# Layer 2's messages in two float32r parts instead of three bf16 parts, in a four-layer graph network

## The chip, the cores and the metric

The kernel runs on one core of a Trainium2 chip. The metric is the device time of one execution in microseconds; of several executions the median is taken. A core has a TensorE for matmuls, a VectorE, a ScalarE and a GpSimd for elementwise work, and queues of transfers (here all issued by SyncE) that move data between the core's own memory and the chip's large one. Each engine works through its instructions in the order in which the program lists them.

## What is computed

64 graphs of 256 nodes with 256 features each run through four layers. Each layer normalises its input, applies a ReLU, and adds its result to the input. Layers 0, 1 and 3 are forms of masked graph attention. Layer 2, which the change rewrites in part, is a gated graph network of three steps; `A` holds zeros and ones.

```python
# --- layer 2 (adj_preln) ---
h = jnp.maximum(_layernorm(x, axis=-1), 0.0)
x = x + _L2_gnn_ref(h, adj, L2_gnn_weight, L2_gnn_w_ih, L2_gnn_w_hh, L2_gnn_b_ih, L2_gnn_b_hh)
# ...
    def _gru_cell(inp, h, w_ih, w_hh, b_ih, b_hh):
        gi = inp @ w_ih.T + b_ih
        gh = h @ w_hh.T + b_hh
        # split in three; r, z sigmoids
        n = jnp.tanh(i_n + r * h_n)
        return (1.0 - z) * n + z * h
# ...
    A = (adj != 0).astype(x.dtype)
    h = x
    for i in range(3):
        m = jnp.einsum('bnd,de->bne', h, weight[i])
        aggr = jnp.einsum('bst,bsd->btd', A, m)
        h = _gru_cell(aggr, h, w_ih, w_hh, b_ih, b_hh)
    return h
```

## The kernel before

Two graphs form a pair, and the 32 pairs are the unit of work (T = 4 blocks of 128 nodes, P = 128, N = D = 256, N2 = 512). The Python program first collects tasks, each with an engine (or several to choose from), an assumed duration and the buffers it reads and writes. A planner then orders all tasks of all pairs by simulating the engines with these assumed durations, so that tasks of several pairs interleave on each engine. Among tasks that could begin at the same time, keys decide: in the kernel before, one key per layer for TensorE, for the transfers and for the others.

Layer 2 multiplies the adjacency first (`A.T h`) and folds the layer's weight into the input weights of the gates (`giT`). In the kernel before, the fp32 state `h` is split in three bf16 parts whose sum is `h`, so that each product with the zeros and ones of the adjacency is exact. The upper half of a float32 is a bf16, and so the stationary operand is read in place with a stride (`upper`).

```python
    def layer2(xt, p):
        at, hT, h = norm_relu_T(xt, p, tokens=True)
        am = buf("mask")
        add(
            (V, dve2(T * N), lambda: nc.vector.tensor_scalar(am(), at().bitcast(I32), 0.0, None, ALU.not_equal), True),
            reads=[hT, at], writes=[am],
        )
        at_o = lambda b, o: tok(b(), N2)[:, o, :]


        def upper(ap):
            return ap.bitcast(BF).rearrange("p (i h) -> p i h", h=2)[:, :, 1]

        def chunk_of(ap, mixed, t, o):
            if mixed:
                return upper(ap).rearrange("p (m x) -> p x m", x=2 * T)[:, T * o + t]
            return tok(upper(ap))[:, t, o * P : (o + 1) * P]

        def messages(h):
            rest = [w4(), w4()]
            add(
                (V, dve(T * N), lambda: nc.vector.tensor_tensor(
                    rest[0](), h(), upper(h()), ALU.subtract), True),
                reads=[h], writes=[rest[0]],
            )
            add(
                (V, dve(T * N), lambda: nc.vector.tensor_tensor(rest[1](), rest[0](), upper(rest[0]()), ALU.subtract), True),
                reads=[rest[0]], writes=[rest[1]],
            )
            aT = w4()
            for o in range(2):
                ps = bank()

                def product(o=o, ps=ps):
                    for g in range(2):
                        for i in range(3):
                            part = (h, *rest)[i]
                            for c in range(2):
                                t = 2 * g + c
                                mm(
                                    ps()[:, g * N : (g + 1) * N], chunk_of(part(), h.mixed, t, o), tok(am(), N)[:, t, :],
                                    start=i == 0 and c == 0, stop=i == 2 and c == 1,
                                )

                add((PE, 1.38, product), reads=[h, *rest, am], writes=[ps], claims=[aT])
                add(
                    evict(N2, lambda o=o: at_o(aT, o), ps),
                    reads=[ps], writes=[(aT, o)],
                )
            return aT
```

The gates are fp32 matmuls of 512 columns; each step has 24 of them:

```python
            def gate(us, terms, c0, o, claims=()):
                ps = bank()

                def do():
                    n = 0
                    for w, src in terms:
                        for k in range(2):
                            mm(ps(), w[:, k, c0 : c0 + P], wide(src, k), start=n == 0, stop=n == 2 * len(terms) - 1)
                            n += 1

                add((PE, us, do), reads=[*(src for _, src in terms), HH, *([GI[l]] if len(terms) > 1 or terms[0][0] is not whhT else [])], writes=[ps], claims=claims)
                return ps

            # ...
            for o in range(2):
                ps = gate(1.72, ((whhT, hT),), (4 + o) * P, o, [r, hn])
                # ... hn = 0.5 * ps + bias, on ScalarE or VectorE
            aT = messages(h)
            both = ((whhT, hT), (giT[:, l], aT))
            for o in range(2):
                ps = gate(3.44, both, o * P, o, [r])
                # ... tanh on ScalarE, then hn = (r + 1) * hn on VectorE
            for o in range(2):
                ps = gate(1.72, ((giT[:, l], aT),), (4 + o) * P, o, [u])
                # ... hn = tanh(ps + hn); u = hT - hn
            for o in range(2):
                ps = gate(3.44, both, (2 + o) * P, o)
                # ... tanh on ScalarE; u = 0.5 * (r + 1) * u + hn on VectorE
            hT = u
            h = w4()
            if by_dma(l, p):          # all pairs but the last one
                turn_chunks(u, h)
            # ... in the last pair: eight transposes on TensorE
```

After each step the new state lies with features on the partitions and must be turned. This goes through 32x32 transposes on VectorE and one write and four reads of the large memory, which leave the features in a mixed order:

```python
    def turn_chunks(src, dst):

        e = w4()
        add(
            (V, 1.8, lambda: nc.vector.transpose(
                e().rearrange("p (b i x) -> p b x i", b=4, i=32), src().rearrange("p (x b j) -> p b x j", b=4, j=32))),
            reads=[src], writes=[e],
        )
        through_dram(e, dst)
        dst.mixed = True

    # ...
    def through_dram(e, eT):

        d = buf("turn")
        add((SP, 0.6, lambda: nc.sync.dma_start(d(), e())), reads=[e], writes=[d], latency=4.6)
        for b in range(4):
            add(
                (SP, 0.55, lambda b=b: nc.sync.dma_start(
                    eT()[32 * b : 32 * b + 32, :].rearrange("p (a w) -> p a w", a=4),
                    d()[:, b * N : (b + 1) * N].rearrange("(a j) w -> j a w", a=4))),
                reads=[d], writes=[(eT, b)], latency=3.8,
            )
```

Of the kernel before, what the change touches and what calls it, by code (L numbers as in the profile page):

```python
# [9 lines left out]
FP = mybir.dt.float32  # L10
BF = mybir.dt.bfloat16
I32 = mybir.dt.int32
# [4 lines left out]
P = 128  # L17
# [17 lines left out]
class Task:  # L35
    __slots__ = ("pair", "forms", "bufs", "rank", "layer", "before", "after", "waits", "begin", "end", "engine", "latency", "rest", "key", "index")


class Plan:
# [14 lines left out]
    SPARE, GRAIN = 6, 0.001  # L54
# [4 lines left out]
    PERIOD, REST = 896, 0  # L59
    ON_PE = (-1435, -211, 9269, -4344)  # L60
    ON_SP = (6322, 2165, 5264, -1155)
    OTHERS = (224, 368, 701, 3083)

    def __init__(self, slots, spare):
        self.slots, self.spare = slots, spare
        self.pairs = []
        self.layer, self.rank = 0, None
# [4 lines left out]
    def add(self, forms, reads=(), writes=(), latency=0.0, claims=()):  # L72
# [11 lines left out]
        t.layer = self.layer  # L84
# [24 lines left out]

    def order(self):  # L110
# [11 lines left out]
        for t in reversed(every):  # L122
            t.rest = max((x.rest + 0.2 for x in t.after), default=0.0) + min(f[1] for f in t.forms) + t.latency
            base = t.rank[0] * self.PERIOD - t.rest * self.REST + t.rank[1] * 1e-4
            engine = t.forms[0][0]
            t.key = base + (self.ON_PE if engine == "PE" else self.ON_SP if engine == "SP" else self.OTHERS)[t.layer]
# [3 lines left out]
        free = {}  # L130
# [5 lines left out]
        while ready:  # L136
            best = None
            for t in ready:
# [8 lines left out]
                else:  # L147
                    for form in t.forms:
                        engine = form[0]
                        begin = max(start, free.get(engine, 0.0), free.get("port", 0.0) if len(form) > 3 else 0.0)  # L150
                        for x in t.before:
                            hop = self.HOP[x.engine] + (engine == "SP") * self.MARGIN if x.engine != engine else self.SAME[x.engine]
                            begin = max(begin, x.end + hop)
                        back = self.BACK.get(engine, 0.0) if len(t.forms) > 1 else 0.0
                        key = (round((begin + back) / self.GRAIN), t.key, t.index)
                        if best is None or key < best[0]:
                            best = (key, t, form, begin)
# [1070 lines left out]
```

## Time and profile before

| | |
|---|---|
| time, median of 3 | 3664.25 us (3661.39 to 3668.29) |
| span of the profiled execution | 3661.3 us, 55666 instructions |
| TensorE's granted clock, mean | 0.993 |
| moved by transfers | 687.78 MB, mean 188 GB/s |

A row of the profile names the line of the kernel, the engine, the operation, the tile written and the tiles read, the shape, and the number of instructions; then the busy microseconds, the mean duration of one in ns, and the idle time of the engine before them with what ended it. L929 is the matmul of `messages`, L951 that of `gate`, L695 layer 0's scores, L745 its context, L1113 layer 3's product, L863 layer 1's product, and L538 the transposes ahead of each layer. Matmul records carry a modelled end, so that the sum of their durations is more than the time that passes; for what one costs, the step from one start to the next is read. A float32 matmul appears as two records, a bf16 matmul as one.

The groups of VectorE and ScalarE that the change touches, with the durations that serve as measures for the new instructions:

```profile
L621 DVE STREAM_TRANSPOSE w<-w 128x1024 f32<-128x1024 f32 x93 | 192.5, 2070 | 1.1
L916 DVE TENSOR_TENSOR w<-w 128x1024 f32<-128x1024 f32 x96 | 118.4, 1234 | 2.5
L911 DVE TENSOR_TENSOR w<-w 128x1024 f32<-128x1024 f32 x96 | 117.3, 1222 | 5.4 <-ACT w L316 2.8 <-DMA w<-turn 1.5 <-ACT w L513 1.1
L985 DVE TENSOR_TENSOR w<-ps,w 128x512 f32<-128x512 f32 x192 | 128.0, 678 | 71.1 <-PE ps L951 70.9
L1128 DVE STREAM_TRANSPOSE w<-w 128x512 f32<-128x512 f32 x62 | 43.6, 703 | 11.4 <-ACT w L316 11.3
L316 ACT COPY w<-ps 128x512 f32<-128x512 f32 x547 | 302.7, 579 | 132.7 <-PE ps L929 52.6 <-PE ps L745 37.7 <-PE ps L675 13.4
```

### The profile page before, as it was taken

Reading aid. Unit: us, or ns where it says so; the run is one execution under the profiler, and the core shown is the slowest. Engines: PE = TensorE matmul, PEld = TensorE weight load, DVE = VectorE, ACT = ScalarE, POOL = GpSimd, SP = SyncE. Lnnn points to the kernel's source line nnn. Section 1 sums busy time; section 2 is a strip of 40 time slices with the busy share of each in tenths; the row PEclk is TensorE's granted clock in tenths of the full one; section 3 lists DMA queues with packets and bytes.
Section 4 is the critical chain, followed back from the end, with each engine's and each line's share of the span. In section 5 each row is a group of like instructions: output and inputs, shape, how many; then the busy total and the mean of one; then the engine's idle time right before and its main releaser. Section 6 shows DMA issues by size and latency. Waiting matters only on the chain.

```text
span 3661.3 us, 55666 instructions
## 1 busy us (share of the span) xinstructions
PE 3600.6 (98%) x16369; PEld 2042.1 (56%) x16369; DVE 2951.6 (81%) x8204; ACT 2587.2 (71%) x6995; POOL 428.1 (12%) x455
## 2 busy tenths in 40 slices
PE   8999999999999999999999999999999999999996
PEld 5655555555555555555555555555555555555553
DVE  7886788888888888888888878888888888788655
ACT  6986566787666777667787667776667776677545
POOL 2000111101111011111011111011110011110100
PEclk9999999999999999999999999999999999999997
DMA  7863567876667866667766567766678666677433
GB/s 223 232 190 98 166 191 196 230 200 190 179 178 198 236 190 183 177 183 212 222 190 177 178 195 220 205 188 180 176 195 236 193 185 172 186 209 223 128 99 104
DMA packets 544144, 687.78 MB, mean 188 GB/s; under 512 B 86112, under 2 KB 463072, under 8 KB 543840
## 3 DMA queue, kind: packets, MB, share of 16 engines
q1 hardware_dynamic: 543840, 684.21, 66.3%
q8 instruction: 131, 2.15, 0.3%
q14 instruction: 173, 1.42, 0.1%
HBM read 394.28 MB, written 281.35 MB: 185 GB/s over the span
## 4 chain that ended last, share of the span: by engine, by line
PE 95%; DVE 2%; ACT 2%; DMA 1%; issue 0%; SPq 0%; POOL 0%; POOLq 0%; DVEq 0%; ACTq 0%
PE ps L951 53%; PE ps L929 7%; PE ps L567 6%; PE ps L675 6%; PE ps L695 4%; PE ps L1113 3%; PE ps L863 3%; PE ps L1061 3%; PE ps L745 3%; PE ps L801 3%; PE ps L538 3%; ACT w L651 1%; PE ps L411 0%; DVE w L602 0%; DVE w L644 0%
## 5 line engine op out<-in xcount | busy, mean ns | idle before, releaser
L951 PE MATMUL ps<-w,whhT 128*128 128x512 f32 x2304 | 1076.2, 596 | 1.4 <-ACT w L316 1.4
L951 PE MATMUL ps<-w,giT 128*128 128x512 f32 x2304 | 1066.3, 594 | 0.0
L651 ACT ACTIVATE w<-w,mx 128x256 f32<-128x256 f32 x1536 | 757.1, 496 | 1.5 <-DVE mx L644 1.5
L951 PEld LDWEIGHTS ps<-w,giT 128*128 128x128 f32 x2304 | 432.5, 190 | 530.6 <-issue 502.1
L951 PEld LDWEIGHTS ps<-w,whhT 128*128 128x128 f32 x2304 | 422.4, 190 | 463.9 <-issue 441.8
L602 DVE STREAM_TRANSPOSE w<-w 128x1024 f32<-128x1024 f32 x380 | 467.7, 1236 | 40.2 <-ACT w L726 29.9
L644 DVE CUSTOM_DVE_ANT_0 w<-ps,mask 128x256 f32<-128x256 f32 x1024 | 376.1, 417 | 44.2 <-PE ps L695 44.1
L316 ACT COPY w<-ps 128x512 f32<-128x512 f32 x547 | 302.7, 579 | 132.7 <-PE ps L929 52.6
L994 POOL TENSOR_TENSOR w<-w,w 128x512 f32<-128x512 f32 x95 | 131.0, 1379 | 1821.4 <-ACT w L989 1403.0
L726 ACT ACTIVATE w<-w,rz 128x256 f32<-128x256 f32 x688 | 299.5, 500 | 15.3 <-DVE rz L719 15.3
L973 ACT ACTIVATE w<-ps,brz 128x512 f32<-128x512 f32 x192 | 130.3, 679 | 252.7 <-PE ps L951 252.7
L513 ACT ACTIVATE w<-x,rs 128x256 f32<-128x256 f32 x394 | 211.2, 595 | 117.0 <-DVE rs L505 116.6
L651 ACT ACTIVATION_READ_ACCUMULATOR w<-w,mx 128x1 f32 x1536 | 290.7, 189 | 0.0
L978 DVE SCALAR_TENSOR_TENSOR w<-w,w 128x512 f32<-128x512 f32 x192 | 132.8, 692 | 181.4 <-ACT w L973 181.2
L929 PEld LDWEIGHTS <-w 128*128 128x128 bf16 x2304 | 246.3, 128 | 43.5 <-issue 28.4
L929 PE MATMUL ps<-mask,w 128*128 128x256 bf16 x2304 | 268.2, 273 | 2.2 <-DVE w L916 2.2
L989 ACT ACTIVATE w<-w,bih_sb 128x512 f32<-128x512 f32 x192 | 135.2, 717 | 166.6 <-DVE w L985 166.4
L1091 ACT ACTIVATE w<-w,f 128x256 f32<-128x256 f32 x512 | 228.5, 499 | 7.7 <-DMA w<-row 7.7
L550 ACT ACTIVATE w<-ps 128x512 f32<-128x512 f32 x187 | 104.3, 595 | 168.8 <-PE ps L538 168.8
L1001 ACT ACTIVATE w<-ps,brz 128x512 f32<-128x512 f32 x192 | 129.2, 673 | 126.7 <-PE ps L951 126.4
L486 DVE BATCH_NORM_STATS2 st<-x 128x6 f32<-128x256 f32 x512 | 189.6, 412 | 10.8 <-DMA x<-in_x_dram 7.4
L644 DVE CUSTOM_DVE_ANT_0 w<-w,mask 128x256 f32<-128x256 f32 x512 | 188.3, 420 | 9.9 <-ACT w L1091 9.9
(113 smaller groups left out, 5118.4 us busy)
## 6 DMA issues: line engine op xcount, KB each, us to landing
turn<-w SPq DMA_DIRECT2D x473, 512.0 KB
w<-turn SPq DMA_DIRECT2D x1892, 128.0 KB
w<-in_adj_dram SPq DMA_DIRECT2D x128, 512.0 KB
w<-row SPq DMA_DIRECT2D x64, 512.0 KB
x<-in_x_dram SPq DMA_DIRECT2D x64, 256.0 KB
out_dram<-x SPq DMA_DIRECT2D x64, 256.0 KB
turn<-w SPq DMA_DIRECT2D x62, 256.0 KB
w<-turn SPq DMA_DIRECT2D x248, 64.0 KB
```

Of the source, the lines that this page charges most:

```text
L316: (A, act(n), lambda: nc.scalar.copy(dst(), src())),
L486: nc.vector.bn_stats(st()[:, t, :], tok(xt())[:, t, :])
L513: nc.scalar.activation(tok(xn())[:, t, :], tok(xt())[:, t, :], func, bias=rs()[:, 1, t : t + 1], scale=rs()[:, 0, t : t + 1])
L567: mm(ps()[:, c * D : (c + 1) * D], chunk(src, k, 2 * g + c), rhs[:, k, :], start=k == 0, stop=k == 1)
L602: add((V, dve(T * N), lambda: nc.vector.transpose(blocks(), blocks())), writes=[e])
L644: nc.vector.tensor_tensor_reduce(row, src, mask, scale, 3.0e38, ALU.add, ALU.min, mn)
L651: nc.scalar.activation(row(e, r), row(e, r), AF.Exp, bias=mn()[:, r : r + 1], scale=-1.0, accum_out=zs()[:, z0(r) : z0(r) + 1])
L675: mm(ps(), w[:, k, o * P : (o + 1) * P], wide(hT, k), start=k == 0, stop=k == 1)
L726: op(row, row, rz()[:, r : r + 1])
L929: mm(ps()[:, g * N : (g + 1) * N], chunk_of(part(), h.mixed, t, o), tok(am(), N)[:, t, :], start=i == 0 and c == 0, stop=i == 2 and c == 1,)
L951: mm(ps(), w[:, k, c0 : c0 + P], wide(src, k), start=n == 0, stop=n == 2 * len(terms) - 1)
L1091: nc.scalar.activation(dst, src, AF.Prelu, bias=f()[:, t, D + h : D + h + 1], alpha=ALPHA)
```

## The change

The state is split in two parts of float32r, a four-byte format with a shorter mantissa: a rounded copy (`high`) and the remainder (`low`), whose sum is again `h`. A message product so takes two parts instead of three. Both parts are written to tiles of their own, one graph (512 columns) at a time, in such an order that every stationary operand of 128 columns lies contiguous; the turn's layout is changed to fit, and its one strided transpose becomes two. The adjacency's zeros and ones become float32r too.

```diff
     def layer2(xt, p):
         at, hT, h = norm_relu_T(xt, p, tokens=True)
-        am = buf("mask")
-        add(
-            (V, dve2(T * N), lambda: nc.vector.tensor_scalar(am(), at().bitcast(I32), 0.0, None, ALU.not_equal), True),
-            reads=[hT, at], writes=[am],
-        )
+        ams = [buf("part") for g in range(2)]
+        for g in range(2):
+            add(
+                (V, dve2(N2), lambda g=g: nc.vector.tensor_scalar(
+                    ams[g](), at()[:, g * N2 : (g + 1) * N2].bitcast(I32), 0.0, None, ALU.not_equal), True),
+                reads=[hT, at], writes=[ams[g]],
+            )
         at_o = lambda b, o: tok(b(), N2)[:, o, :]
 
 
-        def upper(ap):
-            return ap.bitcast(BF).rearrange("p (i h) -> p i h", h=2)[:, :, 1]
-
-        def chunk_of(ap, mixed, t, o):
-            if mixed:
-                return upper(ap).rearrange("p (m x) -> p x m", x=2 * T)[:, T * o + t]
-            return tok(upper(ap))[:, t, o * P : (o + 1) * P]
+        def half_of(h, g):
+            if h.mixed:
+                return h().rearrange("p (a g y i) -> p g a y i", a=4, g=2, i=32)[:, g]
+            return h()[:, g * N2 : (g + 1) * N2]
+
+        def chunk_of(ap, mixed, c, o):
+            y = 2 * o + c if mixed else 2 * c + o
+            return ap[:, y * P : (y + 1) * P]
+
+        def part_of(ap, h):
+            return ap.rearrange("p (y a i) -> p a y i", a=4, i=32) if h.mixed else ap
 
         def messages(h):
-            rest = [w4(), w4()]
-            add(
-                (V, dve(T * N), lambda: nc.vector.tensor_tensor(
-                    rest[0](), h(), upper(h()), ALU.subtract), True),
-                reads=[h], writes=[rest[0]],
-            )
-            add(
-                (V, dve(T * N), lambda: nc.vector.tensor_tensor(rest[1](), rest[0](), upper(rest[0]()), ALU.subtract), True),
-                reads=[rest[0]], writes=[rest[1]],
-            )
             aT = w4()
-            for o in range(2):
+            for g in range(2):
+                high, low = buf("part"), buf("part")
+                of = h if h.mixed else (h, g)
+                add(
+                    [
+                        (A, act(N2), lambda g=g, high=high: nc.scalar.copy(part_of(high(), h), half_of(h, g))),
+                        (V, dve(N2), lambda g=g, high=high: nc.vector.tensor_copy(part_of(high(), h), half_of(h, g)), True),
+                    ],
+                    reads=[of], writes=[high], claims=[low],
+                )
+                add(
+                    (V, dve(N2), lambda g=g, high=high, low=low: nc.vector.tensor_tensor(
+                        part_of(low(), h), half_of(h, g), part_of(high(), h).bitcast(FP), ALU.subtract), True),
+                    reads=[of, high], writes=[low],
+                )
                 ps = bank()
 
-                def product(o=o, ps=ps):
-                    for g in range(2):
-                        for i in range(3):
-                            part = (h, *rest)[i]
+                def product(g=g, ps=ps, high=high, low=low):
+                    for o in range(2):
+                        for i, part in enumerate((high, low)):
                             for c in range(2):
-                                t = 2 * g + c
                                 mm(
-                                    ps()[:, g * N : (g + 1) * N], chunk_of(part(), h.mixed, t, o), tok(am(), N)[:, t, :],
-                                    start=i == 0 and c == 0, stop=i == 2 and c == 1,
+                                    ps()[:, o * N : (o + 1) * N], chunk_of(part(), h.mixed, c, o), tok(ams[g](), N)[:, c, :],
+                                    start=i == 0 and c == 0, stop=i == 1 and c == 1,
                                 )
 
-                add((PE, 1.38, product), reads=[h, *rest, am], writes=[ps], claims=[aT])
-                add(
-                    evict(N2, lambda o=o: at_o(aT, o), ps),
-                    reads=[ps], writes=[(aT, o)],
+                add((PE, 0.96, product), reads=[high, low, ams[g]], writes=[ps], claims=[aT])
+                add(
+                    evict(N2, lambda g=g: tok(aT(), N2)[:, :, g * N : (g + 1) * N], lambda ps=ps: tok(ps(), N)),
+                    reads=[ps], writes=[(aT, g)],
                 )
             return aT
...
     def turn_chunks(src, dst):
 
         e = w4()
-        add(
-            (V, 1.8, lambda: nc.vector.transpose(
-                e().rearrange("p (b i x) -> p b x i", b=4, i=32), src().rearrange("p (x b j) -> p b x j", b=4, j=32))),
-            reads=[src], writes=[e],
-        )
+
+        def blocks():
+            for g in range(2):
+                nc.vector.transpose(
+                    e().rearrange("p (b g o c i) -> p g o c b i", b=4, g=2, o=2, c=2)[:, g],
+                    src().rearrange("p (o g c b j) -> p g o c b j", o=2, g=2, c=2, b=4)[:, g],
+                )
+
+        add((V, 2 * dve(N2), blocks), reads=[src], writes=[e])
         through_dram(e, dst)
         dst.mixed = True
```

The buffers are divided anew (count, shape, type, and a reserve kept for the oldest pair):

```diff
         "x": (5, [P, T * D], FP, 0),
-        "w4": (28, [P, T * D], FP, 9),
+        "w4": (24, [P, T * D], FP, 5),
+        "part": (12, [P, N2], FR, 0),
         "f3": (2, [P, T, E3], FP, 0),
-        "mask": (6, [P, T * N], BF, 1),
+        "mask": (5, [P, T * N], BF, 0),
         "ps": (8, [P, 512], FP, 2),
-        "w2": (6, [P, N2], FP, 2),
+        "w2": (3, [P, N2], FP, 2),
         "st": (4, [P, T, 6], FP, 1),
...
-        "turn": (8, [P, T * N], FP, 0),
-        "turn2": (4, [P, N2], FP, 0),
+        "turn": (8, [P, T * N], FP, 3),
+        "turn2": (4, [P, N2], FP, 1),
```

The planner gets a key for each of some twenty stages and each kind of engine, and it knows that tasks that use TensorE in parts (32 or 64 rows or columns at a time) change its mode: a change is assumed to cost 0.19 us, and among tasks that could begin at the same time those of the present mode are preferred. `HOLD`, with which such tasks could be made to wait for others of their kind, is zero.

```diff
-    SPARE, GRAIN = 6, 0.001
+    SPARE, GRAIN = 5, 0.001
     SLOW, MARGIN = 1.4, 0
     BACK = {"DVE": 0.3, "POOL": 1.1}
 
 
-    PERIOD, REST = 896, 0
-    ON_PE = (-1435, -211, 9269, -4344)
-    ON_SP = (6322, 2165, 5264, -1155)
-    OTHERS = (224, 368, 701, 3083)
+    PERIOD = 1901
+
+
+    KEYS = {
+        ("io", "SP"): -29236, ("w", "SP"): 6718, ("w", "on"): -18369, ("w", "PE"): 8658, ("0n", "on"): -3731,
...
-                    for form in t.forms:
-                        engine = form[0]
-                        begin = max(start, free.get(engine, 0.0), free.get("port", 0.0) if len(form) > 3 else 0.0)
-                        for x in t.before:
-                            hop = self.HOP[x.engine] + (engine == "SP") * self.MARGIN if x.engine != engine else self.SAME[x.engine]
-                            begin = max(begin, x.end + hop)
-                        back = self.BACK.get(engine, 0.0) if len(t.forms) > 1 else 0.0
-                        key = (round((begin + back) / self.GRAIN), t.key, t.index)
-                        if best is None or key < best[0]:
-                            best = (key, t, form, begin)
+                    fit.append((t, start))
+                    if t.mode != "full" and max(start, self.data(t, "PE")) <= free.get("PE", 0.0) + 0.3:
+                        tiled[t.mode] += 1
+            for t, start in fit:
+                for form in t.forms:
+                    engine, key = form[0], t.key
+                    data = max(start, self.data(t, engine))
+                    begin = max(data, free.get(engine, 0.0), free.get("port", 0.0) if len(form) > 3 else 0.0)
+                    at = begin
+                    if engine == "PE":
+                        if t.mode != now:
+                            hold = self.HOLD[self.MODES.index(t.mode) - 1] if t.mode != "full" else 0.0
+                            if hold and tiled[t.mode] < 2:
+                                at = max(at, data + hold)
+                            begin = max(at, free.get("PE", 0.0) + self.SWITCH)
+                        elif t.mode != "full":
+                            key -= 1e6
+                    back = self.BACK.get(engine, 0.0) if len(t.forms) > 1 else 0.0
+                    key = (round((at + back) / self.GRAIN), key, t.index)
+                    if best is None or key < best[0]:
+                        best = (key, t, form, begin)
             _, t, form, begin = best
             engine, us, do = form[:3]
+            if engine == "PE":
+                now = t.mode
...
-                add((PE, 1.11, scores), reads=[qT, kT], writes=banks, claims=[*es, *mns])
+                add((PE, 0.88, scores), reads=[qT, kT], writes=banks, claims=[*es, *mns], mode="rows")
...
-            add((PE, 1.93, context), reads=[(v, g), *pT], writes=[psc], claims=[cT])
+            add((PE, 1.75, context), reads=[(v, g), *pT], writes=[psc], claims=[cT], mode="columns")
...
-            add((PE, 1.86, product), reads=[*eT, (f, 2 * g), (f, 2 * g + 1)], writes=[pso], claims=[oT])
+            add((PE, 1.75, product), reads=[*eT, (f, 2 * g), (f, 2 * g + 1)], writes=[pso], claims=[oT], mode="halves")
```

The assumed duration of a transpose falls from 0.118 to 0.11 us. The computation of layers 0, 1 and 3 is unchanged; the addition of layer 2's result to `x` follows the new layout.

## The prediction

> **What bounds the kernel now.** I read the page's busy shares first, then the busy time by stretch, the waits of TensorE, and TensorE's own timeline of one stretch in the middle. The shares (busy us, share of the span, instructions):
>
> ```profile
> PE 3600.6 (98%) x16369; PEld 2042.1 (56%) x16369; DVE 2951.6 (81%) x8204; ACT 2587.2 (71%) x6995; POOL 428.1 (12%) x455
> ```
>
> A busy TensorE of 98% could still be an average over full and starved stages, so I cut the span into stretches (columns: us, then busy us of each engine and its instructions, granted clock, DMA share, GB/s):
>
> ```profile
> 0.00:100.00 100.00, 82.92 (x474) 53.30 (x475) 77.05 (x289) 68.56 (x198) 20.80 (x28) 0.95 0.78 223
> ...
> 653.94:764.99 111.05, 111.05 (x507) 62.87 (x507) 92.18 (x256) 80.65 (x220) 13.05 (x14) 1.00 0.70 195
> 1431.31:1542.36 111.05, 111.05 (x507) 62.87 (x507) 91.96 (x256) 80.65 (x220) 13.11 (x14) 1.00 0.69 196
> ...
> 3541.00:3600.00 59.00, 54.22 (x171) 27.05 (x167) 32.00 (x64) 15.86 (x25) 4.34 (x4) 1.00 0.14 45
> 3600.00:3661.00 61.00, 28.34 (x137) 17.24 (x137) 31.86 (x117) 37.95 (x113) 3.15 (x5) 0.69 0.49 147
> ```
>
> The two middle stretches are each one pair of graphs: the same work comes back every 111.05 us, with the same 507 matmul records, and TensorE is never idle in them. VectorE has 19 us of slack per pair, ScalarE 30. There are 32 pairs: 32 x 111.05 = 3553.6 of 3661.3 us. The other 107.7 us are the weights' preparation, filling and draining. TensorE's longest waits confirm it: a few long ones, which the timelines of the start and the end place there.
>
> ```profile
> PE ps L1113 <- DMA w<-turn: 15.2, 3, 8.3
> PE ps L538 <- ACT w L513: 11.8, 2, 7.9
> ```
>
> So in the steady state only TensorE's own work counts. The records' durations include a pipelined end; what a record costs is the step from one start to the next, which the timeline shows (start, us, line, count):
>
> ```profile
> 1568.41 2.78 PE L929 MATMUL ps<-mask,w 128*128 128x256 bf16 x24
> 1571.03 1.88 PE L951 MATMUL ps<-w,whhT 128*128 128x512 f32 x4
> 1572.84 1.93 PE L745 MATMUL ps<-w,w 128*32 128x256 f32 x32
> 1574.71 1.98 PE L951 MATMUL ps<-w,whhT 128*128 128x512 f32 x4
> 1576.53 1.88 PE L951 MATMUL ps<-w,giT 128*128 128x512 f32 x4
> ```
>
> The 24 bf16 matmuls of one message step run from 1568.41 to 1571.03: 2.62 us, 109.2 ns each. That happens three times per pair: 7.86 us of 111.05. The 32 column-tiled ones show something else: the plain group before them should hand over after 1.72 us (as 1600.99 to 1602.71 does elsewhere in that timeline) but takes 1.81, and the group after takes 1.82. A lone tiled task costs 0.19 us of mode changes.
>
> **What the Trainium skill says.** "FP8 and Floating Point Precision", section TensorE Precision Notes: true FP32 takes four passes, and there is a reduced-precision FP32 that reads four bytes and keeps fewer mantissa bits. The trace agrees on the first: layer 1's fp32 product, 8 matmuls of 256 columns, takes 3.56 us in one pair (starts to starts), 445 ns each, 4.07 times the bf16 109.2. No float32r matmul is in the trace before; that it takes one pass is what I infer. "TensorE: Matmul & The Clock Gate", Back-to-back issue gap: N/2.4 + 2.5 ns warm, 109.2 for 256 columns; the bf16 steps agree exactly. The same page, LDWEIGHTS: 128 columns load in 128/1.2 = 107 ns, and the faster weight load has no gain for four-byte elements; so a float32r load may just fit beside its matmul. The nearest thing in the trace is the transpose of 128x128 f32, whose load-and-multiply pairs follow each other every 109 ns (8 from 1600.12 to 1600.99), so a single-pass load of four-byte data keeps that rate. "TensorEngine Tiling (Array Packing)", Key Properties: a change of tiling mode drains TensorE; the 0.19 us above agree.
>
> **The change part by part.**
> *Messages on TensorE.* Before: 3 parts x 2 chunks x 2 outputs x 2 graphs = 24 matmuls. After: 2 parts, so 16. At 109.2 ns this is 1.75 us instead of 2.62; the kernel's own planner books 0.96 us per 8, or 120 ns each. I take 112, near the transposes' rate with a little for the loads: 16 x 0.112 = 1.79, a saving of 0.83 per step, 2.49 per pair, 2.49 x 32 = 80 us. All of it is on the path, as TensorE has no idle time to absorb it. At 109.2 it would be 84 us, at 120 it is (7.86 - 48 x 0.120) x 32 = 67.
>
> *VectorE and ScalarE.* Removed per message step: two subtractions of 1024 columns, median 1.22 us, and the strided turn, median 2.04 us. Added: two subtractions of 512 (0.68, as the 512-column tensor_tensor from PSUM), two transposes of 512 (0.70, as layer 3's), and two rounding copies of 512, which ScalarE may take (0.58, as its PSUM copies). Three times per pair: VectorE 92.0 - 13.4 + 8.3 = 87 us, ScalarE 80.7 + 3.5 = 84. Both stay some 20 us under the new period; none of this counts in the steady state. VectorE falls to about 80% of a 108.5 us period. The mask of the adjacency, now in four-byte halves, I take as even.
>
> *Order.* TensorE already never waits in the middle, so new keys can't shorten that except by placing tiled tasks of the same mode side by side. There are 8 tiled tasks per pair (4 scores, 2 contexts, 2 of layer 3): 8 x 0.19 = 1.5 us per pair, 49 us in all. But a scores task takes 4 of 8 PSUM banks and the planner keeps 2 spare for all but the oldest pair, the holds are 0, and the preference only decides ties: I expect about one saved change in sixteen, 0.1 us per pair, 3 us.
>
> *Fill and drain.* 58 us of TensorE are idle in the first 200 and the last 120 us. The searched keys may better this, and a shorter chain ahead of the last pair's messages (2 x 1.22 becomes 0.58 + 0.68) helps a little: 4 us, a judgement, with 12 either way.
>
> *Buffers.* Four wide tiles fewer (28 to 24), twelve half-width parts more, wide reserve 9 to 5. The parts take over two wide temporaries per step, and the mask (two parts for the whole of layer 2). Neutral, with a risk.
>
> Sum: 3664 - 80 - 3 - 4 = 3577 us.
>
> **Rivals.** (1) float32r moves four-byte columns at half rate, as fp32's single records do (429 ns for 512 columns in the timeline: 0.84 ns a column, twice bf16's 0.43). Then 16 x 0.217 = 3.47 us per step, 0.85 more than now, and the time is 3664 + 82 - 7 = about 3739. For it speaks that every four-byte record in this trace goes at that step; against it that fp32 has to carry two halves of the moving number, and a single-pass format need not, and that the planner books 120 ns. I give it 5%. (2) The weight load becomes the bound: four-byte stationaries don't hide under 107 ns of streaming, and a pair takes 150 ns. Then the saving is (7.86 - 7.2) x 32 = 21 us: 3636. The f32 loads of the gates last 190 ns against 143 for bf16, which speaks for it; the transposes' 109 ns speak against. 8%. (3) The new order starves TensorE: the bound passes to a wait, most likely the turned chunks' way through memory or a free wide tile. One microsecond a pair costs 32 us and halves the gain: about 3609. That the old order reached zero idle, and that VectorE is relieved, speak against it; the four tiles fewer and the smaller reserves speak for it. 15%. (4) The opposite: tiled tasks pair up well and save 0.7 us a pair, 22 us: 3555. 12%.
>
> **Range and chances.** The main case is 3577 with about 14 us of spread from the matmul's step (109 to 120: 3573 to 3590) and the fill. Rivals 3 and 4 widen it to 3546 and 3610; 1 and 2 lie above and take most of the tenth there. The 2% line is 3664.25 x 0.98 = 3591. The main case is below it nearly always, rival 4 wholly; a step of 120 ns with nothing won elsewhere would sit at the line. So 0.71 faster by over 2%, 0.24 within, 0.05 slower, which is rival 1.
>
> **What would show it.** The message matmuls appear as 1536 records (96 x 16) of 256 columns, float32r, a step of 109 to 120 ns; 32 or more records per step would mean passes, 217 ns rival 1, 150 rival 2. The middle repeats every 108 to 109 us with TensorE busy throughout and VectorE near 87 us; a period with TensorE under 107 busy out of 109 is rival 3, and the waits would name who held it. The gates' groups keep 1.72 us. Fewer lone tiled tasks in the timeline is rival 4. The prediction is wrong if the period doesn't fall by 2 to 3 us, or if the fill and drain move by more than 15.

## The result, and the profile after

| | before | after |
|---|---|---|
| time, median of 4 runs each | 3663.14 us (3661.39 to 3668.29) | 3580.49 us (3574.28 to 3581.33) |
| ratio, 95% interval | | 0.9767 (0.9753 to 0.9781) |
| span of the profiled execution | 3661.3 us | 3572.5 us |
| period: one pair of graphs in the middle | 111.05 us | 108.68 us (108.77 counted from other pairs) |
| fill and drain: span less 32 periods | 107.6 us | 94.8 us (91.9) |
| changes of TensorE's mode per pair | 15.9 | 13.25 |

Here and below the period is the start of layer 1's first product (L863 before, L913 after) of pair 29, less that of pair 13, over 16. It needs such a mean, as the new order repeats only every few pairs, and not exactly. In four of the reorderings below no period settles at all: counted from the 7th to the 15th pair on, it lies between 106.5 and 118.0 us. For these the time is read, and TensorE's idle time over the same 16 pairs. The mode changes, to and from tiles of 32 or 64 rows or columns, are counted over these pairs too.

TensorE is still the bound. The busy shares of the changed kernel's page:

```profile
PE 3520.7 (99%) x15601; PEld 1990.1 (56%) x15601; DVE 2802.2 (78%) x8499; ACT 2614.9 (73%) x7012; POOL 454.3 (13%) x509
```

There are 768 matmul records fewer: the third part of the messages. Its stretches (us; busy us and instructions of TensorE, weight loads, VectorE, ScalarE and GpSimd; clock; DMA share; GB/s):

```profile
0.00:100.00 100.00, 86.74 (x485) 56.66 (x486) 79.49 (x285) 73.51 (x216) 21.09 (x28) 0.98 0.84 238
...
1506.19:1724.02 217.83, 217.08 (x966) 122.34 (x965) 175.54 (x531) 162.43 (x436) 28.18 (x31) 1.00 0.71 199
...
3452.50:3512.50 60.00, 56.97 (x200) 30.73 (x199) 38.90 (x103) 33.97 (x85) 4.29 (x5) 0.97 0.49 141
3512.50:3572.50 60.00, 35.87 (x157) 20.38 (x155) 33.44 (x110) 35.81 (x106) 5.64 (x7) 0.77 0.44 132
```

The second stretch is two pairs. TensorE idles 0.75 us in it, where it never idled before; VectorE is busy 87.8 us per pair, where it was 92, and ScalarE 81.2. The last 120 us hold 27.2 us of idle TensorE against 37.4 before.

TensorE's timeline around two message products that follow each other (start, us, line, count):

```profile
1636.63 0.27 PE L817 MATMUL ps<-ident,f 128*4 128x128 f32 x1
1636.65 4.07 PE L987 MATMUL ps<-part,part 128*128 128x256 f32 x32
1640.56 1.88 PE L1010 MATMUL ps<-w,whhT 128*128 128x512 f32 x4
```

The one transpose takes its usual 0.11 us, so the 32 products fill 1636.74 to 1640.56: 119.4 ns each, in one record each. (The first record of a float32r group starts early, beside the group before; its start is not to be read as its turn.) The groups of the new instructions (count, then busy us, mean ns, idle before):

```profile
L987 PEld LDWEIGHTS ps<-part,part 128*128 128x128 f32 x1536 | 195.7, 193 | 42.0 <-issue 23.7 <-DVE part L945 6.7 <-ACT part L971 3.4
L977 DVE TENSOR_TENSOR part<-w,part 128x512 fp32r<-128x512 f32 x192 | 135.7, 734 | 32.3 <-ACT part L971 31.6
L663 DVE STREAM_TRANSPOSE w<-w 128x512 f32<-128x512 f32 x186 | 120.5, 686 | 0.4
L971 ACT CAST part<-w 128x512 fp32r<-128x512 f32 x178 | 102.1, 615 | 0.4 <-DMA w<-turn 0.2
```

A load takes 193 ns on average, nearly as a gate's fp32 load (190); the low part 734 ns, the transposes 686, and ScalarE took 178 of the 192 rounding copies at 615.

### The profile page after: what moved, and what is told of

Same layout as the page of the kernel before. It is cut to its first block, busy times and chain, and to the rows that moved or that the text cites. A ratio compares the mean times of both kernels' runs of the same rounds, so it can differ in the third digit from the quotient of the medians.

```text
span 3572.5 us, 54870 instructions
## 1 busy us (share of the span) xinstructions
PE 3520.7 (99%) x15601; PEld 1990.1 (56%) x15601; DVE 2802.2 (78%) x8499; ACT 2614.9 (73%) x7012; POOL 454.3 (13%) x509
## 4 chain that ended last, share of the span: by engine, by line
PE 82%; ACT 7%; DVE 6%; DMA 3%; issue 1%; SPq 1%; POOL 1%; DVEq 0%; ACTq 0%; POOLq 0%
PE ps L1010 45%; PE ps L719 6%; PE ps L607 6%; PE ps L987 4%; PE ps L740 3%; PE ps L1128 3%; PE ps L848 3%; PE ps L577 3%; PE ps L1183 3%; PE ps L792 2%; PE ps L913 2%; ACT w L695 2%; ACT w L1160 1%; DVE w L642 1%; DMA x<-in_x_dram 1%; DVE w L688 1%
## 5 line engine op out<-in xcount | busy, mean ns | idle before, releaser
L354 ACT COPY w<-ps 128x512 f32<-128x512 f32 x519 | 291.1, 581 | 307.0 <-PE ps L719 90.6
L538 POOL TENSOR_SCALAR rs<-mv 128x4 f32<-128x4 f32 x129 | 41.2, 319 | 1973.8 <-DVE mv L527 1953.9
L772 ACT ACTIVATE w<-w,rz 128x256 f32<-128x256 f32 x606 | 266.2, 501 | 2.2 <-DVE rz L765 2.1
L987 PE MATMUL ps<-part,part 128*128 128x256 f32 x1536 | 222.2, 298 | 9.7 <-DVE part L945 4.9
L1056 POOL TENSOR_TENSOR w<-w,w 128x512 f32<-128x512 f32 x87 | 111.8, 1285 | 909.5 <-ACT w L1051 540.4
L1160 ACT ACTIVATE w<-w,f 128x256 f32<-128x256 f32 x512 | 220.3, 499 | 4.6 <-DMA w<-row 4.5
L987 PEld LDWEIGHTS ps<-part,part 128*128 128x128 f32 x1536 | 195.7, 193 | 42.0 <-issue 23.7
L688 DVE CUSTOM_DVE_ANT_0 w<-w,mask 128x256 f32<-128x256 f32 x512 | 197.7, 426 | 8.5 <-ACT w L1160 8.2
```

The source lines that it names most:

```text
L354: (A, act(n), lambda: nc.scalar.copy(dst(), src())),
L688: nc.vector.tensor_tensor_reduce(row, src, mask, scale, 3.0e38, ALU.add, ALU.min, mn)
L772: op(row, row, rz()[:, r : r + 1])
L987: mm(ps()[:, o * N : (o + 1) * N], chunk_of(part(), h.mixed, c, o), tok(ams[g](), N)[:, c, :], start=i == 0 and c == 0, stop=i == 1 and c ...
L1160: nc.scalar.activation(dst, src, AF.Prelu, bias=f()[:, t, D + h : D + h + 1], alpha=ALPHA)
```

## Experiments

### What a float32r product costs

The step is 119 ns, not 109 as in bf16. Is that the format, or the new arrangement of the product? The parts and the adjacency were made bf16, all else kept (two bf16 parts leave out the last bits of the state):

```diff
-        "part": (12, [P, N2], FR, 0),
+        "part": (12, [P, N2], BF, 0),
 ...
```

> The changed kernel with its two message parts and the adjacency in bf16 instead of float32r; order, layout and number of matmuls stay, and what two bf16 parts cannot hold of the state is left out. Theory (the 120 ns step comes from the four-byte format, by its load or its streaming): the step falls from 120 to 109 ns, the period from 108.92 to about 108.4 us, the time by 48 x 0.0108 x 32 = 17 us to about 3563. Rival (the step comes from the new arrangement of the product: one graph at a time, two outputs in turn, contiguous stationaries): the step stays at 120 and the time near 3580.

Measured: 3562.47 us (one run), period 108.29. Timeline, and the records of the line (duration min/median/max):

```profile
1632.82 3.66 PE L987 MATMUL ps<-part,part 128*128 128x256 bf16 x32
1636.31 1.88 PE L1010 MATMUL ps<-w,whhT 128*128 128x512 f32 x4
```

```profile
L987 PEld LDWEIGHTS <-part x1536: 94/98/152, 137.7 to 3490.2; 128*128 128x128 bf16 x192
```

3.49 us for 32: 109.1 ns. The ten nanoseconds belong to the four-byte format. Next, its load or its streaming? Half the loads over the same columns (half of the blocks are left out, the two outputs fall together):

```diff
-                            for c in range(2):
-                                mm(
-                                    ps()[:, o * N : (o + 1) * N], chunk_of(part(), h.mixed, c, o), tok(ams[g](), N)[:, c, :],
+                            mm(
+                                ps(), chunk_of(part(), h.mixed, i, o), ams[g](),
 ...
```

> The changed kernel with each pair of 256-column float32r products replaced by one of 512 columns, so with half of the stationary loads over the same number of streamed columns; the sums are no longer the reference's, as half of the blocks are left out and the two outputs fall together. Theory L (the load of a four-byte stationary does not hide under 107 ns of streaming): a 512-column step takes 215 to 218 ns, 24 of them 5.2 us per pair instead of 5.76, period about 108.35, time about 3562. Theory S (float32r streams at 0.47 ns a column): a step takes 240 ns and the period stays at 108.9, time near 3580.

Measured: 3575.8 us (one run), period 108.85, a median step of 231 ns, most steps between 224 and 236. The timeline, where one transpose of 0.11 us stands ahead of 16 products:

```profile
1637.92 0.27 PE L817 MATMUL ps<-ident,f 128*4 128x128 f32 x1
1637.95 3.92 PE L986 MATMUL ps<-part,part 128*128 128x512 f32 x16
1641.71 1.88 PE L1009 MATMUL ps<-w,whhT 128*128 128x512 f32 x4
```

Neither theory holds: a 512-column product is not at 215 to 218 (half of a gate's record, or two bf16 products), and it is cheaper than two of 256 columns, which take 239. The period didn't fall, as TensorE idles 0.6 us per pair here instead of 0.3.

The third run asks what the contiguous layout is for. The parts were interleaved, so that a stationary operand's columns lie 16 bytes apart (in the kernel before it was 32 bytes in the turned tiles, and 4 in the tiles of the first message step):

```diff
-            return ap[:, y * P : (y + 1) * P]
+            return ap.rearrange("p (m y) -> p y m", y=4)[:, y]
 ...
-            return ap.rearrange("p (y a i) -> p a y i", a=4, i=32) if h.mixed else ap
+            return ap.rearrange("p (a i y) -> p a y i", a=4, i=32) if h.mixed else ap.rearrange("p (m y) -> p y m", y=4)
```

> The changed kernel, in its order, with the two parts laid so that the four stationary blocks of a part interleave: a stationary operand's 128 columns lie 16 bytes apart, as in the kernel before, instead of contiguous; the writes of the parts take the same stride. Theory C (contiguous stationaries are what keeps a float32r product at 120 ns, the load of strided four-byte columns being slower): a step of 140 ns or more, period 109.7 or more, time over 3610. Rival N (the layout of a stationary does not matter, as it did not for the strided bf16 parts before, 109 ns): a step of 117 to 121 ns, period within 0.4 of 108.7, time 3570 to 3590.

Measured: 3770.53 us (one run), period 115.01. Records of the line in the changed kernel and in this one, this one's timeline, and groups:

```profile
L987 PEld LDWEIGHTS ps<-part,part x1536: 186/192/333, 136.4 to 3502.9; 128*128 128x128 f32 x192
```

```profile
L987 PEld LDWEIGHTS ps<-part,part x1536: 307/329/339, 138.8 to 3699.6; 128*128 128x128 f32 x192
```

```profile
1632.66 1.88 PE L1010 MATMUL ps<-w,giT 128*128 128x512 f32 x4
1634.01 4.16 PE L987 MATMUL ps<-part,part 128*128 128x256 f32 x16
1638.09 1.95 PE L1183 MATMUL ps<-w,f 128*64 128x256 f32 x16
```

```profile
L977 DVE TENSOR_TENSOR part<-w,part 128x512 fp32r<-128x512 f32 x192 | 214.6, 1151 | 50.7 <-ACT part L971 49.7
L971 ACT CAST part<-w 128x512 fp32r<-128x512 f32 x178 | 187.4, 1143 | 0.2
```

Theory C holds by far: the median load grows from 192 to 329 ns and the median step from 120 to 233. (The four gate products take their 1.72 us to 1634.38, so the 16 take 3.71 us, 232 ns each.) A message step so takes 16 x 0.233 = 3.73 us, more than the 2.62 of three bf16 parts: without the new layout two parts lose to three. Of the 6.33 us that the period grows, the steps make 48 x 0.114 = 5.5. TensorE idles 0.5 us more, to which the longer writes may add (1151 and 1143 ns instead of 734 and 615), and stretches at half the granted clock, of which more below, cost some 0.6 us. By this estimate the terms make 6.6, a little too much.

So the load can set the step: here only its layout was changed on TensorE's side. Whether it sets it in the contiguous layout as well isn't shown. There, steps of 117 to 118 ns go with loads of 188 and steps of 120 with 192, but which of the two follows the other can't be told. And half of the 231 ns of a 512-column product is 115.5: if that is streaming, six of the ten ns above bf16 belong to the streaming and only four to the load.

### Messages and order apart

The new messages under the old planner, with the old keys:

```diff
-            t.key = t.rank[0] * self.PERIOD + t.rank[1] * 1e-4 + self.KEYS.get((t.stage, kind), 0.0)
+            t.key = t.rank[0] * self.PERIOD + t.rank[1] * 1e-4 + keys[layer]
 ...
-                        if t.mode != now:
+                        if False:
```

> The float32r messages and the new buffers, under the old planner: keys per layer as before, no account of mode changes, the old assumed durations and reserves of the small buffers. Theory (the message step makes 68 us, the order some 15 of fill and drain): period 108.9 to 109.3, time 3590 to 3600. Rival (the order is what makes the fewer wide tiles work): TensorE idles by a microsecond or more per pair, time 3620 or more. Second rival (the order brought nothing of its own): 3575 to 3585.

Measured: 3713.29 us, ratio 1.013 (1.0113 to 1.0147), period 112.05. The first rival holds: the change's messages and buffers in the old order are slower than the kernel before, and TensorE idles 1.4 us per pair. TensorE's waits (us in total, times, longest):

```profile
PE ps L794 <- DMA w<-turn: 19.1, 15, 4.8
PE ps L579 <- DVE w L560: 10.8, 1, 10.8
PE ps L609 <- ACT w L356: 9.7, 14, 2.5
...
PE ps L742 <- DVE mx L690: 9.1, 23, 0.5
```

L794 is layer 0's context, which waits for turned weights, and L742 its scores, which wait for the VectorE operation that frees their banks. Neither is touched by the change. Their records take 4.80 and 5.38 us per pair from start to start, where they took 3.73 and 4.30. And the other way round, the old messages with the old number of wide tiles under the new planner:

```diff
-        "w4": (24, [P, T * D], FP, 5),
-        "part": (12, [P, N2], FR, 0),
+        "w4": (28, [P, T * D], FP, 9),
 ...
-        ams = [buf("part") for g in range(2)]
+        am = buf("mask")
```

> The three bf16 parts and the old turn of the kernel before, with its wide tiles, under the new planner and its keys per stage. Theory (the message step alone makes the gain of the steady state, and the keys and mode preference only fill, drain and a few mode changes): period 110.7 to 111.1 us, fill and drain near 87 us instead of 108, time 3630 to 3645, a ratio of 0.99 to 0.996. Rival (the keys were found for the new messages and serve no other): fill and drain of 108 or more and idle TensorE in the middle, time 3664 or more.

Measured: 3735.23 us, ratio 1.0193 (1.0176 to 1.021), with 2.1 us of idle TensorE per pair: both exchanges lose. (This is the median of three executions; a fourth took 4180.32 us at a mean granted clock of 0.877 and is left out.) So the keys and reserves belong to a list of tasks. To compare fairly they were searched anew for each, by trial against the planner's own assumed durations.

> As the kernel of the new messages under the old planner (keys per layer, no account of modes, old assumed durations), but with its thirteen keys and its reserves searched anew for the new list of tasks. Theory (the message step makes the gain, and the loss under the old keys was only that they belonged to another list of tasks): period 108.7 to 109.6, time 3575 to 3600, as the changed kernel. Rival (the stages' keys and the account of modes are needed for the gain): period 110.5 or more, time 3630 or more.

```diff
-    ON_PE = (-1435, -211, 9269, -4344)
-    ON_SP = (6322, 2165, 5264, -1155)
-    OTHERS = (224, 368, 701, 3083)
+    ON_PE = (-2758, 637, 4867, -6314)
+    ON_SP = (-2179, -3357, -7126, -5413)
+    OTHERS = (17943, 11663, 1063, 2941)
```

Measured: 3607.73 us, ratio 0.9843 (0.9829 to 0.9858), period 109.06, fill and drain 114.0, 16 mode changes per pair. A stretch of its middle:

```profile
1944.00:2388.00 444.00, 443.58 (x1982) 249.46 (x1984) 365.05 (x1099) 319.88 (x860) 59.17 (x64) 1.00 0.67 195
```

TensorE idles 0.1 us per pair again. This is the message step by itself, with as many mode changes as before: 111.05 - 109.06 = 1.99 us per pair, 64 us. TensorE is full in both, so that only its own work can make the difference. The theory's period holds. The time lies above what the theory said, as fill and drain did not shrink. The same for the old messages under the new planner (keys and reserves alone changed):

> As the kernel of the old messages under the new planner, with its keys per stage and reserves searched anew for the old list of tasks, from the exchanged keys on. Theory (the new planner has little to give of its own, as TensorE never idled in the middle; a search over some fifty keys need not even find the old order again): period 110.8 to 111.6, time 3640 to 3690. Rival (the finer keys are worth the larger part of the gain, whatever the messages): time 3600 or less.

Measured: 3669.34 us, ratio 1.0014 (1.0007 to 1.0021), within the theory's range. TensorE idles 0.8 us per pair in the middle, where it never idled in the kernel before. The new planner gave the old messages nothing as far as the search went. A longer search may find more.

The changed kernel without the account of modes alone:

```diff
 ...
-                        elif t.mode != "full":
-                            key -= 1e6
 ...
-                add((PE, 0.88, scores), reads=[qT, kT], writes=banks, claims=[*es, *mns], mode="rows")
+                add((PE, 1.11, scores), reads=[qT, kT], writes=banks, claims=[*es, *mns], mode="rows")
 ...
```

> The changed kernel with its keys, but a planner that knows no mode changes (no preference for tasks of the present mode, no assumed cost of a change, and the old longer durations of the tiled tasks in its place). Theory (the account of modes brings the 16 to 13.25 changes per pair, 0.28 us, and little else): 15 to 16 changes per pair, period about 109.0, time 3580 to 3595. Rival (the order hangs on the account, as the kernels with exchanged keys hang on theirs): TensorE waits, period 110 or more, time 3630 or more.

Measured: 3645.25 us, ratio 0.9935 (0.9918 to 0.9951), 14.9 mode changes. The rival's time holds: 65 us more than the changed kernel, or 2 us per pair, can't come from one and a half mode changes of some 0.1 us; most of the loss is a worse order. TensorE idles 1.0 us per pair instead of 0.3. In one stretch TensorE idles 10.9 us, in the next 1.9:

```profile
1944.00:2388.00 444.00, 433.06 (x1881) 242.48 (x1880) 360.40 (x1079) 324.26 (x868) 60.20 (x65) 0.99 0.68 193
2388.00:2832.00 444.00, 442.08 (x1975) 248.88 (x1977) 355.47 (x1066) 332.42 (x889) 53.65 (x62) 1.00 0.72 203
```

Last, an attempt to better both kernels: the changed one with its keys and reserves searched on, which by the planner's assumed durations ends earlier.

> The changed kernel with its keys per stage and reserves searched on from where they stood. Theory (some of the 0.3 us of idle TensorE per pair and of the 95 us of fill and drain can still go): 5 to 10 us under the changed kernel, 3568 to 3576. Rival (the planner's assumed durations are no longer close enough to order by them at this grain): 3580 to 3600, or no better than the changed kernel.

```diff
-        ("1n", "on"): 783, ("1n", "SP"): -19498, ("1n", "PE"): -22885, ("1", "on"): -14680, ("1", "PE"): -13623,
 ...
+        ('1n', 'on'): 7785,
+        ('1n', 'SP'): -28808,
+        ('1n', 'PE'): -30474,
+        ('1', 'on'): 9072,
+        ('1', 'PE'): -3703,
 ...
```

(All 60 keys were moved; five are shown.) Measured: 3736.96 us, ratio 1.0193 (1.0178 to 1.0208), outside both the theory's range and the rival's 3580 to 3600, but no better than the changed kernel, as the rival also allowed. TensorE idles 2.1 us per pair in the middle, and its mean granted clock is 0.979 instead of 0.995. Its longest waits are for ScalarE and for turned tiles:

```profile
PE ps L625 <- ACT w L600: 26.1, 14, 9.2
PE ps L700 <- ACT w L743: 20.9, 6, 17.7
PE ps L961 <- ACT w L944: 19.8, 3, 10.6
...
PE ps L840 <- DMA w<-turn: 8.4, 4, 4.4
```

The attempt failed. Which assumed duration misled the planner isn't known.

### How much slack VectorE has

The change takes some 4 us per pair from VectorE, which idles 19 to 22. Does that count? The order was held, and subtractions that nothing reads were put behind each low part, in the same task:

```diff
+            for i in range(4):
+                nc.vector.tensor_tensor(spent, wq_sb[:, 0, :], wk_sb[:, 0, :], ALU.subtract)
```

> The changed kernel in its own order, with four subtractions of 256 columns more on VectorE behind each low part (into a tile that nothing reads): some 0.37 us each, 8 x 3 per pair, about 9 us, which puts back more VectorE work than the change took away per pair (VectorE from some 87 to some 96 us of 108.7). Theory (in the steady state TensorE's work alone counts, and the relief of VectorE is worth nothing there): period 108.7 to 109.5, time 3575 to 3610, most of it from low parts that come later. Rival (the relief of VectorE was part of the gain): the period returns by 2 us or more towards 111, time 3640 or more.

> As the kernel with four subtractions more behind each low part, but with one: 6 x 0.435 = 2.6 us of VectorE more per pair, order unchanged. Theory (in the changed order TensorE and VectorE hang on each other in turn, so that VectorE's idle time is no slack): period 108.7 + 2.6 = 111.3, time about 3660. Rival (there is slack for small delays, and only the ten microseconds overran it): period under 109.3, time under 3600.

(The second has `range(1)`.) And the kernel before, with eight of them behind its last part:

> The kernel before, in its order, with eight subtractions of 256 columns more behind the last part of each message step: 24 x 0.435 = 10.4 us of VectorE more per pair, the same as in the changed kernel with its four. Theory (the hanging on each other is of these planned orders in general): the period grows from 111.05 by 8 to 11 us, time 3920 to 4010. Rival (the order before, with no idle TensorE, had slack on VectorE, and the changed one has used it up): the period grows by under 5 us, time under 3820.

| one run each | VectorE work added per pair | period | growth | time |
|---|---|---|---|---|
| changed kernel | 6 x 0.445 = 2.7 us | 109.46 | 0.78 | 3593.25 |
| changed kernel | 24 x 0.435 = 10.4 us | 118.60 | 9.92 | 3862.34 |
| kernel before | 24 x 0.428 = 10.3 us | 117.71 | 6.65 | 3881.86 |

None of the three theories holds as it was put. The small load cost less than a third of itself, near its rival's 109.3; the large one overshot even its rival; the kernel before lies between its theory and its rival. The changed kernel takes nearly two microseconds; 7.8 more then cost 9.1. The kernel before absorbed 3.6 of 10.3.

Not all of the 9.92 us is waiting. Where TensorE has waited, the granted clock can stand at half for a while. Here is the changed kernel with four subtractions after a wait of 3.86 us, and then the clock of the same stretch (third column from the end):

```profile
2051.68 3.78 PE L993 MATMUL ps<-part,part 128*128 128x256 f32 x16 [3.86 <-DVE part L946]
2055.26 3.15 PE L1016 MATMUL ps<-w,giT 128*128 128x512 f32 x4
2058.24 1.89 PE L608 MATMUL ps<-wo_sb,w 128*128 128x256 f32 x8
```

```profile
2051.00:2057.80 6.80, 6.12 (x19) 4.59 (x20) 3.81 (x7) 1.66 (x3) 0.00 (x0) 0.50 0.76 246
```

The four gate products take 2.98 us (to 2058.24) instead of 1.72, and in the whole run 258 of the 292 steps between message products in such stretches are about 213 ns, and none outside them. The 16 pairs hold 21 of these stretches, of 3.4 or 6.8 us, nearly all within 9 us of a wait of 2.0 to 4.4 us; together they last 5.8 us per pair; at half the clock they cost some 2.9 us per pair, an estimate. TensorE's idle time grows by 5.4 us per pair. In the kernel before with its load the stretches cost some 0.9 us per pair, in the changed kernel with one subtraction nothing. So 6.65 against 9.92 overstates how much better the old order absorbs a load: without the clock it would be some 5.8 against 7.0.

The waits of TensorE, in the changed kernel with four and in the kernel before with eight, show different places:

```profile
PE ps L993 <- DVE part L946: 85.9, 29, 4.4
PE ps L578 <- ACT w L553: 35.3, 32, 9.8
PE ps L993 <- DVE part L966: 19.2, 24, 1.5
```

```profile
PE ps L746 <- DMA w<-turn: 71.7, 26, 3.6
PE ps L864 <- DVE w L1000: 40.2, 25, 1.6
```

In the first, the message products wait for the adjacency's parts (L946) and for the low parts themselves (L966); in the second, layer 0's context waits for its turned weights. VectorE still idles 22.1 us per pair in the first, so its idle time is not slack: engines that work through fixed lists wait for each other in turn, and a delay in one comes back to it. The load was tried at this one place; what it costs elsewhere isn't known.

## Why the prediction was right

The time, 3580, is 3 us from the 3577 predicted, and the range of 3546 to 3610 held. The gain was there, and TensorE's steps made most of it, as predicted. That the sum came out so close is luck: the messages gave 16 us less than predicted, the order some 9 and the fill and drain some 9 more.

**What bounds the kernel.** Right: TensorE's steps set the period before and after.

**Messages, 80 us.** The mechanism was right (one pass, one record per product, no rival of half rate), the size was not: 112 ns was assumed, 119 to 120 measured, so that 48 products take 5.74 us per pair and 2.12 can be saved; the kernel with the old planner and keys of its own shows 1.99, or 64 us. The mis-sized term is the step: the prediction took the fp32 transposes' 109 ns for the rate of four-byte loads. But 109 ns is about what 128 columns take at the gates' 429 ns for 512, so it needn't be a load's rate at all, and the transposes' loads last 142 ns (the mean of L577's in the profile after), the float32r loads 192. These are as long as the gates' fp32 loads of 190 ns, which were cited for the second rival. That rival was given 150 ns and 8%; whether it was true in kind, at 120, isn't settled. The planner's 120 ns was the better number.

**Order, 3 us.** Too small. From the kernel with layer keys of its own to the changed one the period falls from 109.06 to 108.68, 12 us in all (9 with the 108.77 counted from other pairs). 2.75 fewer mode changes at half of 0.19 make an estimated 0.26 us of the 0.38; the remainder isn't resolved. The two products of layer 3 do stand together at times, which the reasoning on PSUM banks had overlooked, as it looked only at the scores.

**Fill and drain, 4 us with 12 either way.** 107.6 to 94.8, 13 us (16 with the other period), within the 12 either way. With the old planner and the new messages it is 114, so this belongs to the new planner or its keys.

64 + 12 + 13 = 89, the difference of the spans, 88.8. The medians differ by 82.7, as the profiled execution was the fastest of its four.

**VectorE and ScalarE, nothing in the steady state.** The loads were right (87 and 84 predicted, 87.8 and 81.2 measured), the reading of their idle time as slack was wrong beyond the first two microseconds. With 10.4 us more on VectorE in that order the time is 3862, and the gain is gone more than three times over. But that is more than twice the 4 us that the change took off VectorE; a load of just these 4, and an order found for a load, weren't tried. So whether the relief of VectorE was needed for the gain isn't shown.

**Buffers, and rival 3.** The changed kernel isn't starved: 0.3 us per pair. But the prediction took order and messages for terms to be added, the one worth 80 and the other 3. They are not: the messages without keys for them cost 50 us (3713 against 3663). A chance of 15% for a starved TensorE looks low beside this: of the four other orders of the new messages tried here, three took at least 64.8 us more than the changed kernel, and one of the two other orders of the old messages took some 70 us more than the kernel before. How much the four missing wide tiles have to do with it wasn't tried apart.

## What to carry to other kernels

When the bound engine never idles, the steps between its starts, times their count, tell what a change of its work is worth; before taking the rate for a new operand format from another record, check what sets that record's step, and whether its load lasts as long. Such an order is fitted to its list of tasks: compare two lists only with orders found for each, and measure the order on the chip, since one that ends earlier by the assumed durations lost by 4% here. Idle time of the other engines is no measure of their slack; a small load added in the fixed order measures it, if the granted clock is watched with it.

## What the runs showed of the hardware that was not expected

A float32r product of 256 columns with contiguous stationary columns steps at 117 to 120 ns, one of 512 columns at 231, where bf16 takes 109 for 256 and one fp32 record 429 for 512. With the stationary columns 16 bytes apart the float32r load takes 329 ns instead of 192 and the step 233. In bf16 the layout did not show in the step: in the kernel before, loads took 143 ns with columns 32 bytes apart and 98 with columns 4 bytes apart, and the contiguous ones of the bf16 run 98, all at 109.

```profile
L929 PEld LDWEIGHTS <-w x2304: 97/143/174, 145.1 to 3575.7; 128*128 128x128 bf16 x192
```

In the stretches at a granted clock of 0.50 the float32r products stepped at 213 to 214 ns with loads of 330. Writes with 16 bytes between elements lengthened VectorE's subtraction from 734 to 1151 ns and ScalarE's copy from 615 to 1143.
